# Dense products of an attention and mixture-of-experts block, issued as four column groups of 32 outputs

## The chip, the core and the metric

The kernel runs on one core of one Trainium2 chip. Its time is the device time of one launch in microseconds (us), as a median of several runs. The core has a matrix engine (PE, with its weight loads listed apart as PEld), a vector engine (DVE), a scalar engine (ACT), GpSimd (POOL) and a queue engine that issues the DMAs (SP). They run side by side and wait for each other through semaphores.

## The reference, cut to what matters

The input x has 4 sequences of 2048 tokens with 512 features, in f32. It is layer-normalized; attention with 16 heads of 32 features and a top-2-of-8 expert layer both read the normalized rows, and both results are added to x:

```python
xn  = _layernorm(x)
qkv = einsum('bnc,dc->bnd', xn, qkv_w) + qkv_b             # q, k, v: dense, 512 x 512 each
attn = softmax(einsum('bhqd,bhkd->bhqk', q, k) * 32**-0.5)
out = einsum('bhqk,bhkd->bhqd', attn, v)
a   = einsum('bnc,dc->bnd', out, proj_w) + proj_b           # dense, 512 x 512
h   = gelu(einsum('bsd,bkde->bkse', xn, W1[idx]) + b1[idx]) # dense, two experts per sequence
o   = einsum('bkse,bkef->bksf', h, W2[idx]) + b2[idx]       # dense
y   = x + a + sum(o, over the two experts) / 2
```

## The kernel before, in words

The work is cut into 1024 units. A unit is one sequence b (4), one group g of four heads (4), one chunk qc of 512 queries (4) and one tile kt of 128 keys (16). The loop over U (L638) writes one unit after the other, and each engine executes what it is given in just this order: the schedule is manual (L216), no scheduler reorders it. LEAD = 22 further units come first, with negative U. The class Plan decides beforehand which dense product goes into which unit.

In a unit PE gets, in this order:

1. `shift` (L533): four bf16 products, 32 contraction rows by 128 outputs, which put minus the row maximum into the banks of the scores.
2. `score` (L542) and `score_max` (L519): eight f32 products with 32 contraction rows and 128 outputs each, one head per 32 rows. Half of them are scores of this unit, half are for the maxima of the unit 22 later.
3. In even units `weigh` (L551): the probabilities of two units times v, eight f32 products of 128 contraction rows and 32 outputs. The four heads write to the four groups of 32 output partitions of one bank. In one even unit out of 16, `add_keys` (L579) follows in the same form: it sums the softmax denominators.
4. In odd units, transposes if there are any (`turn` L361 in f32, `turn_maxima` L616 in bf16, both with 128 rows and 128 outputs), then one dense product by `dense` (L422): q or k (`project_qk`, L405), v (`project_v`, L415), an expert's first (L436) or second layer (L446), or the output projection (L457). Some odd units have no dense product: gaps that Plan spreads over the program.

A dense product fills one bank of 128 partitions x 512 f32. Before the change it is four program matmuls of 128 contraction rows, 128 outputs and 512 columns, one for each quarter of the 512 features:

```python
for d in range(DC):
    nc.tensor.matmul(pp, w[:, d, :], xn[:, d, :], start=(d == 0), stop=(d == DC - 1))
```

One f32 program matmul appears as two weight loads and two matmuls in the trace, so a dense product has 8 loads and 8 matmuls, and a `weigh` has 16 and 16. A bf16 matmul and a transpose appear as one load and one matmul.

`weigh` already has the form that the change gives to the dense products:

```python
for n in range(2):
    for j in range(GH):
        r = rows_of(j)                                   # 32 rows: j*32 to j*32+32
        nc.tensor.matmul(acc[r, :], held["v", ...][:, (kt + n) % TPC, r], pT[u + n][:, j, :],
                         start=(n == 0), stop=(n == 1))
```

The other engines: ACT takes the exponential of the scores (L658), four per unit, and in 32 units the gelu of a whole expert tile with a table load on either side of it (L662). DVE takes the row maxima (L664), four per unit, and sums what `weigh` gives (L567). POOL sums the probabilities for the denominators, one addition per unit (L577, L575 for the first), and does the small steps of the maxima (L610, L612), the division (L629) and a bias (L682). Eight PSUM banks go round among scores, maxima, `weigh` and dense products. Probabilities have four buffers (L219), so ACT can write those of unit U only when PE and POOL are done with those of U-4.

There are 504 dense products of the kind that `dense` and the start (L502 to L505) issue: 8 in the start (q and k of the first head group), 22 in the lead and 474 in the odd units. Eight more at the end (lines 748, 756 and 763) are written apart.

Of the kernel before, what the change touches and what calls it, by code (L numbers as in the profile page):

```python
# [17 lines left out]
P = 128  # L18
HEADS = 16
HD = 32  # L20
GH = P // HD
# [165 lines left out]
def block_kernel(  # L187
# [16 lines left out]
    nc = tc.nc  # L204
    B, N, D = x.shape
    E = Wr.shape[1]
    DC = D // P
# [17 lines left out]
    def bank(name):  # L225
        return ps.tile([P, CH], F32, tag="bank", name=name)

    def rows_of(j):
        return slice(j * HD, (j + 1) * HD)
# [83 lines left out]
    first = pair.tile([B, D], F32, tag="att", name="first")  # L313
# [74 lines left out]
    nc.vector.max_index(chosen, best, scores)  # L388


    kT, qT = {}, {}
    hT, bias, b1s = {}, {}, {}

    def with_bias(dst, src, col, on_dve):
        if on_dve:
            nc.vector.tensor_scalar(dst, src, col, None, ALU.add)  # L396
        else:
            nc.scalar.activation(dst, src, AF.Identity, bias=col)  # L398

    def project_qk(kind, b, g, c, xn, w, on_dve=False):  # L400
        pp = bank(f"{kind}ps_{b}_{g}_{c}")
        t = kv_pool.tile([P, CH], F32, tag=kind, name=f"{kind}T_{b}_{g}_{c}",
                         bufs=2 * NCH if kind == "k" else NCH + 3)
        for d in range(DC):
            nc.tensor.matmul(pp, w[:, d, :], xn[:, d, :], start=(d == 0), stop=(d == DC - 1))  # L405
        col = "qk".index(kind) * DC + g
        with_bias(t, pp, bqkv[:, col : col + 1], on_dve)
        (kT if kind == "k" else qT)[b, g, c] = t

    def project_v(b, n, xn, w, U):  # L410

        c, i = divmod(n, TPC)
        pp = bank(f"vps_{b}_{n}")
        for d in range(DC):
            nc.tensor.matmul(  # L415
                pp, xn[:, d, ts(i, P)], w[:, d, :], start=(d == 0), stop=(d == DC - 1)
            )
        t = pair.tile([P, D], F32, tag="vrow", name=f"v_{b}_{n}")
        nc.vector.tensor_tensor(t, pp, bv_bc, ALU.add)
        later(U + 2, lambda: nc.sync.dma_start(v_dram[b, c][:, i, :], t))  # L420

    def dense(item, U, on_dve):  # L422
        kind, b = item[:2]
        tiles = [held[n] for n in plan.needs(item)]
        if kind in "kq":
            project_qk(kind, *item[1:], *tiles, on_dve=on_dve)
        elif kind == "v":
            project_v(*item[1:], *tiles, U)
        elif kind == "w1":
            c, k, f = item[2:]  # L430
            xn, w = tiles
            if f == 0:
                hT[k] = stream.tile([P, DC, CH], F32, tag="h", name=f"h_{b}_{c}_{k}", bufs=2)
            pp = bank(f"hps_{b}_{c}_{k}_{f}")
            for d in range(DC):
                nc.tensor.matmul(pp, w[:, d, :], xn[:, d, :], start=(d == 0), stop=(d == DC - 1))  # L436
            with_bias(hT[k][:, f, :], pp, b1s[b, k][:, f : f + 1], on_dve)
            if f == DC - 1:
                at = U + 2 if U > 0 or U == -1 else U + 1
                curves[at] = hT[k]  # L440
        elif kind == "w2":
            c, k, i = item[2:]
            w, row = tiles
            pp = bank(f"ops_{b}_{c}_{k}_{i}")
            for f in range(DC):
                nc.tensor.matmul(  # L446
                    pp, hT[k][:, f, ts(i, P)], w[:, f, :], start=(f == 0), stop=(f == DC - 1)
                )
            nc.vector.scalar_tensor_tensor(row, pp, 0.5, row, ALU.mult, ALU.add)
            if k == TOP_K - 1:  # L450
                later(U + 2, lambda: nc.sync.dma_start(part_dram[b, c, i], row))
        else:
            qc, i = item[2:]
            at, w, row = tiles
            pp = bank(f"prps_{b}_{qc}_{i}")
            for g in range(DC):
                nc.tensor.matmul(  # L457
                    pp, at[:, g, ts(i, P)], w[:, g, :], start=(g == 0), stop=(g == DC - 1)
                )
            finish(b, qc, i, pp, row, U)  # L460

    def finish(b, qc, i, pp, row, U):
        tok = qc * CH + i * P
        nc.vector.tensor_tensor(row, pp, row, ALU.add)
        later(U + 2, lambda: nc.sync.dma_start(out[b, tok : tok + P, :], row))
# [31 lines left out]
    for c in range(NCH):  # L497
        xn = load("xq", ("stage", 0, c))
        for i in range(TPC):
            turn(xn, x_first[c][:, i, :], i, f"0_{c}_{i}")  # L500
        nc.sync.dma_start(xn_dram[0, c], xn)
        if c + 1 < NCH:  # L502
            first_norm(c + 1)
        for kind in "kq":
            project_qk(kind, 0, 0, c, xn, held["w" + kind, 0])  # L505


    def place(u):
        rest, kt = divmod(u, NT)
        rest, qc = divmod(rest, NCH)  # L510
        return (*divmod(rest, DC), qc, kt)
# [4 lines left out]
    def later(u, do):  # L516
        waiting.setdefault(u, []).append(do)
# [120 lines left out]
    for U in range(-LEAD, plan.units):  # L638
# [3 lines left out]
        b, g, qc, _ = place(U) if second else (0, 0, 0, 0)  # L642
# [22 lines left out]
        last = U + LEAD  # L665
        if first_pass is not None and last % NT == NT - 1:
            where, n = place(last)[:3], last // NT
# [26 lines left out]
        for step, sb, n in plan.extra.get(U, []):  # L694
# [8 lines left out]
            else:  # L703
                c, i = divmod(n, TPC)
# [6 lines left out]
        for item in plan.items.get(U, []):  # L711
            dense(item, U, curve is not None)
# [13 lines left out]
        for n, c in ((16, NCH - 1), (1, NCH - 2)):  # L726
            if U == plan.units - n:
# [7 lines left out]
                n = DC - 1 if c == NCH - 1 else DC  # L735
# [8 lines left out]
    w = held["wb", ("proj",)]  # L744
    for i in range(TPC):
        pp = bank(f"last2_{i}")
# [6 lines left out]
    for i in range(TPC):  # L753
        pp = bank(f"last1_{i}")
# [58 lines left out]
```

## Time and profile before

| what | value |
|---|---|
| median of 3 runs | 5157.79 us (5157.7 to 5157.85) |
| the profiled execution's own time | 5157.05 us |
| its span | 5155.2 us |
| mean granted PE clock | 0.999 of full speed |
| PE busy | 5076.8 us, 98% of the span |
| POOL busy | 4515.3 us, 88% |
| DVE busy | 3449.7 us, 67% |
| ACT busy | 2520.4 us, 49% |
| matmuls, weight loads | 33924 each |
| HBM traffic | 65 GB/s over the span |

The busy time of PE counts overlapping matmuls once. In the timeline a line gives start, length, engine, line of the kernel, operation, the tiles written and read, contraction rows*outputs, and the count; "idle before" in brackets tells how long the engine sat idle and what ended it. For PEld, idle time is ordinary: a load takes less time than the matmul that it prepares.

### The profile page before, as it was taken

What the parts mean: (1) busy time and instruction counts of PE and PEld (TensorE: products, weight loads), DVE (VectorE), ACT (ScalarE), POOL (GpSimd) and SP (SyncE); (2) the same over time, 40 slices, a digit from 0 to 9 for tenths busy, and PEclk for the clock granted to TensorE, in tenths of its full rate; (3) what the DMA queues carried; (4) which work ended last, traced back from release to release, by engine and by line L of the source; (5) the groups of instructions that cost most, each with busy time, mean ns of one, the idle gap of its engine ahead of it and who ended that gap; (6) DMA issues with size and microseconds to landing.
All of it is one profiled execution on the core that took longest, in us unless ns stands there. A gap on an engine that the chain in (4) does not pass through costs nothing.

```text
span 5155.2 us, 83981 instructions
## 1 busy us (share of the span) xinstructions
PE 5076.8 (98%) x33924; PEld 2028.1 (39%) x33924; DVE 3449.7 (67%) x5495; ACT 2520.4 (49%) x4571; POOL 4515.3 (88%) x1430
## 2 busy tenths in 40 slices
PE   8999999999999999999999999999999999999998
PEld 3333333433333333443333433343333333333343
DVE  5666676766766667666766767766667666666672
ACT  1445545544544545554445454555444454555543
POOL 0699898988999989998999989989999998999992
PEclk9999999999999999999999999999999999999999
DMA  4211112301222212221121221221112211021112
GB/s 164 68 56 50 52 64 79 111 30 38 66 82 68 66 64 78 72 80 44 48 93 46 78 84 52 86 84 58 39 57 87 77 62 58 17 74 34 38 44 78
DMA packets 220580, 338.64 MB, mean 66 GB/s; under 512 B 14364, under 2 KB 129052, under 8 KB 205984
## 3 DMA queue, kind: packets, MB, share of 16 engines
q1 hardware_dynamic: 220192, 333.28, 19.2%
q8 instruction: 266, 4.36, 0.3%
q14 instruction: 122, 1.00, 0.1%
HBM read 249.61 MB, written 83.62 MB: 65 GB/s over the span
## 4 chain that ended last, share of the span: by engine, by line
PE 96%; POOL 2%; ACT 1%; DVE 1%; issue 0%; DMA 0%; SPq 0%; ACTq 0%; POOLq 0%
PE acc L558 18%; PE m L528 17%; PE s L546 17%; PE hps L436 9%; PE ops L446 9%; PE s L538 7%; PE kps L405 5%; PE vps L415 5%; PE qps L405 4%; PE prps L457 4%; POOL psum L577 2%; PE keys L583 1%; ACT L658 1%; PE xt L365 1%; ACT p L658 1%
## 5 line engine op out<-in xcount | busy, mean ns | idle before, releaser
L577 POOL TENSOR_TENSOR psum<-psum,p 128x2048 f32<-128x2048 f32 x882 | 3991.1, 4525 | 240.7 <-ACT p L658 206.3
L664 DVE TENSOR_REDUCE mx<-m 128x1 f32<-128x512 f32 x4096 | 2544.5, 684 | 1074.1 <-PE m L528 1073.3
L658 ACT ACTIVATE p<-s 128x512 f32<-128x512 f32 x4096 | 2121.8, 604 | 1811.6 <-PE m L528 1680.7
L546 PE MATMUL s<-qT,kT 32*128 32x512 f32 x8192 | 1922.5, 588 | 0.0
L528 PE MATMUL m<-kT,qT 32*128 32x512 f32 x8192 | 1908.3, 590 | 2.5 <-DVE h L396 1.4
L528 PEld LDWEIGHTS m<-kT,qT 32*128 32x128 f32 x8192 | 931.4, 184 | 323.0 <-issue 241.7
L558 PE MATMUL acc<-p,v 128*32 128x512 f32 x8192 | 990.1, 599 | 39.2 <-ACT p L658 39.2
L546 PEld LDWEIGHTS s<-qT,kT 32*128 32x128 f32 x8192 | 764.5, 185 | 30.8 <-issue 12.5
L558 PEld LDWEIGHTS acc<-p,v 128*32 128x32 f32 x8192 | 215.4, 109 | 739.1 <-ACT p L658 429.0
L436 PE MATMUL hps<-xf,w 128*128 128x512 f32 x1024 | 472.9, 604 | 0.2 <-ACT p L658 0.2
L446 PE MATMUL ops<-wb_w,h 128*128 128x512 f32 x1024 | 472.8, 604 | 0.2 <-ACT p L658 0.2
L538 PE MATMUL s<-negm,ones_b 32*128 32x512 bf16 x4096 | 420.9, 384 | 5.5 <-ACT p L658 3.5
L538 PEld LDWEIGHTS <-ones_b 32*128 32x128 bf16 x4096 | 108.7, 91 | 804.4 <-issue 797.2
L567 DVE TENSOR_TENSOR sacc<-acc,sacc 128x512 f32<-128x512 f32 x448 | 310.0, 692 | 153.6 <-PE acc L558 153.6
L575 POOL TENSOR_TENSOR psum<-p,p 128x2048 f32<-128x2048 f32 x63 | 284.6, 4517 | 132.8 <-ACT p L658 132.8
L446 PEld LDWEIGHTS ops<-wb_w,h 128*128 128x128 f32 x1024 | 184.0, 189 | 269.2 <-issue 183.7
L436 PEld LDWEIGHTS hps<-xf,w 128*128 128x128 f32 x1024 | 184.0, 189 | 268.8 <-issue 186.0
L398 ACT ACTIVATE h<-hps,b 128x512 f32<-128x512 f32 x115 | 79.2, 688 | 355.8 <-PE hps L436 355.8
L415 PE MATMUL vps<-wb_v,xq 128*128 128x512 f32 x512 | 236.8, 605 | 2.2 <-issue 2.0
L676 DVE RECIPROCAL sums<-sums 128x128 f32<-128x128 f32 x252 | 237.9, 944 | 0.7 <-ACT sums L595 0.7
L405 PE MATMUL kps<-xq,wk 128*128 128x512 f32 x480 | 221.6, 604 | 1.0 <-ACT p L658 0.2
L405 PE MATMUL qps<-xq,wq 128*128 128x512 f32 x480 | 221.5, 604 | 0.1
(89 smaller groups left out, 1839.2 us busy)
## 6 DMA issues: line engine op xcount, KB each, us to landing
xq<-xn_dram SPq DMA_DIRECT2D x64, 1024.0 KB, 5.5
w<-in_W_dram SPq DMA_DIRECT2D x128, 256.0 KB, 3.1
xn_dram<-xq_stage SPq DMA_DIRECT2D x16, 1024.0 KB, 6.4
v_dram<-v SPq DMA_DIRECT2D x64, 256.0 KB, 2.4
xf<-xn_dram SPq DMA_DIRECT2D x16, 1024.0 KB, 6.0
v<-v_dram SPq DMA_DIRECT2D x64, 256.0 KB, 4.3
row<-in_x_dram SPq DMA_DIRECT2D x64, 256.0 KB, 5.8
part_dram<-row SPq DMA_DIRECT2D x64, 256.0 KB, 2.1
```

The costliest lines, as they stand in the source:

```text
L405: nc.tensor.matmul(pp, w[:, d, :], xn[:, d, :], start=(d == 0), stop=(d == DC - 1))
L415: nc.tensor.matmul(pp, xn[:, d, ts(i, P)], w[:, d, :], start=(d == 0), stop=(d == DC - 1))
L436: nc.tensor.matmul(pp, w[:, d, :], xn[:, d, :], start=(d == 0), stop=(d == DC - 1))
L446: nc.tensor.matmul(pp, hT[k][:, f, ts(i, P)], w[:, f, :], start=(f == 0), stop=(f == DC - 1))
L528: nc.tensor.matmul(t, qT[b, g, qc][r, ts(i, P)], kT[b, g, kc][r, :], start=True, stop=True)
L538: nc.tensor.matmul(tiles[j], ones_b[r, :], negm[b, g, qc][r, :], start=True, stop=False)
L546: nc.tensor.matmul(tiles[j], kT[b, g, kt // TPC][r, ts(kt % TPC, P)], qT[b, g, qc][r, :], start=False, stop=True,)
L558: nc.tensor.matmul(acc[r, :], held["v", (b, g, kt // TPC)][:, (kt + n) % TPC, r], pT[u + n][:, j, :], start=(n == 0), stop=(n == 1),)
L567: nc.vector.tensor_tensor(t, acc, t, ALU.add)
L577: nc.gpsimd.tensor_tensor(psums[b, g, qc], psums[b, g, qc], pT[u], ALU.add)
L658: nc.scalar.activation(pT[U][:, j, :], tiles[j], AF.Exp, scale=SCALE)
L664: nc.vector.tensor_reduce(dst, t, AX.X, ALU.max, negate=True)
```

## The change

A new helper `product` issues every dense product of `project_qk`, `project_v` and `dense` as column groups: for each quarter of the contraction, four matmuls, each with 32 columns of the stationary operand and the 32 output partitions that belong to them. The moving operand of the four is the same tile. The number of program matmuls of a product goes from 4 to 16. The order of everything else, on all engines, stays as it was; so do the eight products at the end, the transposes, and the readers of the banks.

```diff
+    def product(pp, terms, last=True, first=True):
+
+        for n, (lhsT, rhs) in enumerate(terms):
+            for j in range(GH):
+                nc.tensor.matmul(
+                    pp[rows_of(j), :], lhsT[:, rows_of(j)], rhs,
+                    start=(first and n == 0), stop=(last and n == len(terms) - 1),
+                )
...
     def project_qk(kind, b, g, c, xn, w, on_dve=False):
...
-        for d in range(DC):
-            nc.tensor.matmul(pp, w[:, d, :], xn[:, d, :], start=(d == 0), stop=(d == DC - 1))
+        product(pp, [(w[:, d, :], xn[:, d, :]) for d in range(DC)])
...
     def project_v(b, n, xn, w, U):
...
-        for d in range(DC):
-            nc.tensor.matmul(
-                pp, xn[:, d, ts(i, P)], w[:, d, :], start=(d == 0), stop=(d == DC - 1)
-            )
+        product(pp, [(xn[:, d, ts(i, P)], w[:, d, :]) for d in range(DC)])
...
     def dense(item, U, on_dve):
...
-            for d in range(DC):
-                nc.tensor.matmul(pp, w[:, d, :], xn[:, d, :], start=(d == 0), stop=(d == DC - 1))
+            product(pp, [(w[:, d, :], xn[:, d, :]) for d in range(DC)])
...
-            for f in range(DC):
-                nc.tensor.matmul(
-                    pp, hT[k][:, f, ts(i, P)], w[:, f, :], start=(f == 0), stop=(f == DC - 1)
-                )
+            product(pp, [(hT[k][:, f, ts(i, P)], w[:, f, :]) for f in range(DC)])
...
-            for g in range(DC):
-                nc.tensor.matmul(
-                    pp, at[:, g, ts(i, P)], w[:, g, :], start=(g == 0), stop=(g == DC - 1)
-                )
+            product(pp, [(at[:, g, ts(i, P)], w[:, g, :]) for g in range(DC)])
```

## The prediction

> **What bounds the kernel.** I read the page first: busy times, then the chain of work that ended last.
>
> ```profile
> PE 5076.8 (98%) x33924; PEld 2028.1 (39%) x33924; DVE 3449.7 (67%) x5495; ACT 2520.4 (49%) x4571; POOL 4515.3 (88%) x1430
> ...
> PE 96%; POOL 2%; ACT 1%; DVE 1%; issue 0%; DMA 0%; SPq 0%; ACTq 0%; POOLq 0%
> PE acc L558 18%; PE m L528 17%; PE s L546 17%; PE hps L436 9%; PE ops L446 9%; PE s L538 7%; PE kps L405 5%; PE vps L415 5%; PE qps L405 4%; PE prps L457 4%; POOL psum L577 2%; PE keys L583 1%; ACT L658 1%; PE xt L365 1%; ACT p L658 1%
> ```
>
> PE carries the chain, and the dense lines (L405 to L457) are 36% of it. So what one dense product costs between its neighbours on PE is what counts. The timeline of weight loads near the end shows a dense product and, right after it, eight packs of four column groups (four of L558, four of L583): as many contraction passes as a dense product, in the form that the change gives it.
>
> ```profile
> 5078.69 0.30 PEld L457 LDWEIGHTS prps<-wb_proj,xl_at 128*128 128x128 f32 x2 [0.76 <-issue]
> ...
> 5082.32 0.10 PEld L538 LDWEIGHTS <-ones_b 32*128 32x128 bf16 x4 [0.76 <-issue]
> ...
> 5083.50 0.16 PEld L558 LDWEIGHTS acc<-p,v 128*32 128x32 f32 x8 [0.76 <-issue]
> 5083.96 0.13 PEld L558 LDWEIGHTS acc<-p,v 128*32 128x32 f32 x4 [0.30 <-issue]
> 5084.39 0.13 PEld L558 LDWEIGHTS acc<-p,v 128*32 128x32 f32 x4 [0.30 <-issue]
> 5084.82 0.13 PEld L583 LDWEIGHTS keys<-p,ones 128*32 128x32 f32 x4 [0.30 <-issue]
> ...
> 5087.07 0.10 PEld L538 LDWEIGHTS <-ones_b 32*128 32x128 bf16 x4 [0.84 <-issue]
> ```
>
> First load to the first load of what follows: 5082.32 - 5078.69 = 3.63 us for the dense product, 5087.07 - 5083.50 = 3.57 us for the packs. Both come after a drain of PE and end with one.
>
> **The change, per product.** From single start times in the trace: (a) First load to the second matmul (or pack): 535 ns dense, 455 ns for `acc`. The first load takes 0.19 us for 128 outputs, 0.11 for 32, and the four small loads run side by side. Saved: 80 ns. (b) After it, matmuls come every 429 ns in both forms. Pace: no change. (c) In a pack the four groups start 6 to 7 ns apart, so the last ends 20 ns later: +20. Sum -60 ns (3631 against 3571). The 3631 hold for 394 products that follow the 32-row scores, and alike for the other positions; the same drain (516 ns from the last matmul's start to the next load) precedes both forms.
>
> A rule speaks against (c). The Trainium skill ("TensorE: Matmul & The Clock Gate", section "Measured speedup vs the span model") has a pack last a matmul plus about 4 ns for each further tile. If that came with each of 8 packs, it would be 8 x 12 = 96 ns, more than the 80 saved: +16 ns per product. The row shows packs at 429 ns, the stagger paid once. I take the row; the rule makes the first rival.
>
> **After transposes.** 45 products follow an f32 transpose directly, 36 a bf16 one. Both are 128 rows x 128 outputs, the tiling of the old products, not of the new ones. For f32 the dense load now starts 54 ns after the last transpose matmul does: no drain. The Trainium skill ("TensorEngine Tiling (Array Packing)", section "Key Properties") says that a change of tiling mode drains PE. No row shows an f32 transpose followed by another tiling, so: a drain costs 516 - 429 = 87 ns beyond the last matmul's own pace after 512 columns; 128 columns take a quarter, 107 ns; 107 + 87 - 54 = +140 ns, net +80 per product. Bounds: 0 (no drain) and 280 (twice); I take 140, nearest to the row. For bf16:
>
> ```profile
> 1477.75 0.23 PEld L620 LDWEIGHTS <-spread 128*128 128x128 bf16 x4 [0.76 <-POOL att L629]
> 1478.19 0.30 PEld L405 LDWEIGHTS kps<-xq,wk 128*128 128x128 f32 x2 [0.21 <-ACT p L658]
> ```
>
> Here 0.44 us pass from the first transpose's load to the dense load, although the tiling is the same; before a 32-row bf16 load it is 0.33 at its usual value. So this place waits already. Bounds: the wait shrinks by 108 ns, or grows by 87; I take no change.
>
> **What lies on the path.** The 474 products in odd units and the 22 in the lead stand in PE's chain. From one `add_keys` to the next are 16 units; with eight products, no gelu and no f32 transposes such a stretch lasts 77.87 us in 15 of 17 cases, and PE has work in all of it, so PE alone sets it. In units with gelu, ACT still waits 0.36 us for PE before its table load, so 0.06 us pass through there too. In the start, 4 pairs of q and k stand between transposes: each saves the load and pays a drain; I count 0. Where POOL is the chain, the gain is lost:
>
> ```profile
> 4948.20 2.08 ACT p L658 x4
> ...
> 4950.41 4.54 POOL psum L577
> ...
> 5051.80 4.56 POOL psum L577
> ...
> 5058.75 3.63 PE prps L457 x8
> ```
>
> From 4950 to 5056 us POOL works without a wait for PE. Six dense products lie there; they gain nothing.
>
> Sum: 496 - 6 = 490, of which 45 follow f32 and 36 bf16 transposes, 409 neither. 409 x 0.0605 = 24.7; 36 x 0.0605 = 2.2; 45 x 0.080 = -3.6: 23.3 us less. From the profiled execution's 5157.05 (span 5155.2 and 1.85 around it) that makes 5133.8; the median of the runs stood 0.7 higher, so 5134.5.
>
> The costs set at nothing: evacuation by ACT and DVE reads the same bank, 20 ns later within a product that ends 60 earlier. 504 x 48 = 24192 more PE instructions are fetched; instruction queues hold 0.4% of the DMA time now. No wait is added: all four groups use one bank, and the reader waits for the last matmul.
>
> **Rivals.** (1) Stagger in each pack, by the rule above: 409 + 36 products at +0.016 and 45 at +0.156 make +14.1 us: 5172. This ends slower. It decides from 10 ns per pack (80 / 8); for it is only the rule, against it the 429 ns of packs in a row.
>
> (2) PE's instruction supply. A pair of units with a product now holds 128 loads and matmuls in 9.57 us, 75 ns each; it would be 176 in 9.51, 54 ns each. If PE's sequencer gave one per 60 ns, each of 474 pairs would take 10.56 us: +498 us, 5630. It decides from 54 ns. For it: nothing so dense runs for long. Against: from 5091.9 us on, 346 instructions ran in 18.3 us (53 ns each) at undisturbed pack pace. If PE's queue holds 64 (the figure of the first page, which no run here shows), they exclude only more than 18.3 / (346 - 64) = 65 ns. The same page's sustained rate of 81 ns for a load and a 128-column matmul would be 40 ns each, an estimate that leaves room.
>
> (3) POOL takes over, half the gain is lost: 11.6 us, 5146. POOL has 88% of the span, but ACT overwrites probabilities 5.2 us or more after POOL has read them, everywhere before 4980 us; eight products per 16 units take only 0.5 us from this, and POOL falls idle again in most of them. Unlikely outside the tail.
>
> (4) The change doesn't do what it says: the small loads don't run side by side for a shared moving tile, and products stay as long as they were; with the drains after transposes, 5158 to 5164.
>
> **How the numbers follow.** Forecast 0.72, within 5124 to 5144.5: the low end has no drain after f32 transposes (6.3) and the shorter wait after bf16 (3.9), the high end twice the drain (6.3), the longer wait (3.1) and 0.6 in the start. Rival (3) 0.06, (4) 0.08, (1) 0.05, (2) 0.05; 0.04 for a larger gain that I don't see. The range 5122 to 5147 takes in the forecast and (3), and a little of the last. A measurement of this kernel tells 0.2%, 10.3 us, from no change. Faster by more: 0.72 + 0.06 + 0.04 = 0.82; within: 0.08; slower: 0.10.
>
> **What would show it.** Right: the first loads of a product as 8 small ones within 0.16 us, packs at 0.43, 3.57 us from first load to the next L538, and stretches with eight plain products at 77.87 - 8 x 0.06 = 77.39 us. For the drain: about 0.19 us instead of 0.05 between the last f32 transpose and the product. Wrong: packs over 0.44 us (1), pauses between packs in odd units only, or loads that trickle (2), ACT waiting for L577 in mid-program (3). The forecast falls if a product's 3.57 us don't come about.

## The result and the profile after

The changed kernel takes 5134.1 us (median of 6 runs, 5133.48 to 5136.19) against 5157.82 us (6 runs, 5154.98 to 5158.59): 23.7 us less, a ratio of 0.9955 with a 95% interval of 0.9944 to 0.9967. The forecast was 5134.5. The profiled execution has a span of 5131.6 us, 23.6 below the one before.

The page's busy times and the head of its chain:

```profile
PE 5054.0 (98%) x46020; PEld 1776.4 (35%) x46020; DVE 3449.0 (67%) x5495; ACT 2516.2 (49%) x4571; POOL 4534.6 (88%) x1430
...
PE 95%; POOL 2%; ACT 1%; DVE 0%; issue 0%; DMA 0%; SPq 0%; ACTq 0%; POOLq 0%
```

12096 more matmuls and as many more weight loads, and yet PE is busy for 22.8 us less: four matmuls of four column groups, which run side by side (a pack), count as the time of one. PE still carries the chain. The timeline of weight loads shows the same output projection near the end that the prediction showed of before:

```profile
5055.06 0.16 PEld L395 LDWEIGHTS prps<-wb_proj,xl_at 128*32 128x32 f32 x8 [0.76 <-issue]
5055.52 0.13 PEld L395 LDWEIGHTS prps<-wb_proj,xl_at 128*32 128x32 f32 x4 [0.30 <-issue]
5055.95 0.13 PEld L395 LDWEIGHTS prps<-wb_proj,xl_at 128*32 128x32 f32 x4 [0.30 <-issue]
...
5058.63 0.10 PEld L536 LDWEIGHTS <-ones_b 32*128 32x128 bf16 x4 [0.84 <-issue]
```

Eight small loads come within 0.16 us, packs follow every 0.43, and 5058.63 - 5055.06 = 3.57 us pass until the next part's load. From single start times it is 3571 ns in nearly all products that follow scores, 3631 before. After f32 transposes the picture is another. The same view around one of them, before and then after:

```profile
813.07 0.42 PEld L365 LDWEIGHTS xt<-ident,xl_normal 128*128 128x128 f32 x4 [0.76 <-ACT p L658]
813.50 0.30 PEld L436 LDWEIGHTS hps<-xf,w 128*128 128x128 f32 x2
```

```profile
804.75 0.42 PEld L365 LDWEIGHTS xt<-ident,xl_normal 128*128 128x128 f32 x4 [0.76 <-ACT p L656]
805.34 0.16 PEld L395 LDWEIGHTS hps<-xf,w 128*32 128x32 f32 x8 [0.17 <-ACT p L656]
```

From the first transpose's load to the product's first load it is 0.43 us before and 0.59 after: the product now waits for the transposes. Measured from the last transpose's start, 54 ns have become 201.

Stretch by stretch (16 units, from one `add_keys` to the next) the two traces differ by 0.48 us where there are eight plain products, by 0.42 where there are seven, and by -0.55, -0.40 and -0.02 in three neighbouring stretches of each of the first three sequences: there the transposes lie, and the kernel is slower than before.

Three differences in the profiled pair belong to the clock of these two executions and not to the change. PE's granted clock became full at 22.2 us before and at 16.9 after, which shortens the start by 2.1 us, and each trace has a spell of half clock of 3.4 us in mid-program (last section) that costs 1.5 us before and 1.7 after. Together they favour the profiled execution of after by some 1.9 us, so 21.7 of its 23.6 us are left for the change.

### The profile page after: what moved, and what is told of

It is laid out like the page before. It is cut to its first block, busy times and chain, and to the rows that moved or that the text cites. A ratio compares the mean times of both kernels' runs of the same rounds, so it can differ in the third digit from the quotient of the medians.

```text
span 5131.6 us, 108175 instructions
## 1 busy us (share of the span) xinstructions
PE 5054.0 (98%) x46020; PEld 1776.4 (35%) x46020; DVE 3449.0 (67%) x5495; ACT 2516.2 (49%) x4571; POOL 4534.6 (88%) x1430
## 3 DMA queue, kind: packets, MB, share of 16 engines
q8 instruction: 361, 5.91, 0.5%
## 4 chain that ended last, share of the span: by engine, by line
PE 95%; POOL 2%; ACT 1%; DVE 0%; issue 0%; DMA 0%; SPq 0%; ACTq 0%; POOLq 0%
PE acc L556 18%; PE m L526 17%; PE s L544 17%; PE ops L395 9%; PE hps L395 9%; PE s L536 7%; PE kps L395 4%; PE vps L395 4%; PE qps L395 4%; PE prps L395 4%; POOL psum L575 2%; PE keys L581 1%; ACT L656 1%; PE xt L365 1%; ACT p L656 1%; PE mt L618 0%
## 5 line engine op out<-in xcount | busy, mean ns | idle before, releaser
L575 POOL TENSOR_TENSOR psum<-psum,p 128x2048 f32<-128x2048 f32 x882 | 4008.6, 4545 | 217.3 <-ACT p L656 182.1
L395 PE MATMUL hps<-xf,w 128*32 128x512 f32 x4096 | 466.0, 595 | 0.2 <-ACT p L656 0.2
L395 PE MATMUL ops<-wb_w,h 128*32 128x512 f32 x4096 | 466.0, 595 | 0.2 <-ACT p L656 0.2
L395 PE MATMUL vps<-wb_v,xq 128*32 128x512 f32 x2048 | 233.0, 595 | 2.3 <-issue 2.0
L395 PEld LDWEIGHTS ops<-wb_w,h 128*32 128x32 f32 x4096 | 120.0, 109 | 317.6 <-issue 229.8
L395 PEld LDWEIGHTS hps<-xf,w 128*32 128x32 f32 x4096 | 120.0, 109 | 317.1 <-issue 232.1
L395 PE MATMUL kps<-xq,wk 128*32 128x512 f32 x1920 | 218.4, 595 | 1.0 <-ACT p L656 0.2
L395 PE MATMUL qps<-xq,wq 128*32 128x512 f32 x1920 | 218.4, 595 | 0.1
```

What stands on the lines that cost most here:

```text
L395: nc.tensor.matmul(pp[rows_of(j), :], lhsT[:, rows_of(j)], rhs, start=(first and n == 0), stop=(last and n == len(terms) - 1),)
L575: nc.gpsimd.tensor_tensor(psums[b, g, qc], psums[b, g, qc], pT[u], ALU.add)
```

## The experiments

All times are medians; ratios are to the kernel before, on the same chip.

**1. The old form after f32 transposes.** Products in units with f32 transposes keep their four wide matmuls (unless a bf16 transpose lies between); all else is as in the changed kernel.

```diff
+    plain = [False]
+
     def product(pp, terms, last=True, first=True):
 
+        if plain[0]:
+            for n, (lhsT, rhs) in enumerate(terms):
+                nc.tensor.matmul(
+                    pp, lhsT, rhs,
+                    start=(first and n == 0), stop=(last and n == len(terms) - 1),
+                )
+            return
...
+        turned = any(step == "turn" for step, _, _ in plan.extra.get(U, []))
+        plain[0] = turned and not (last % NT == 3 and NT < last <= plan.units + 3)
         for item in plan.items.get(U, []):
```

> Products that directly follow f32 transposes (45 of them) keep the old form of 128 outputs, all others are four column groups. Theory: the column form gains 60 ns per product but pays a drain after an f32 transpose, because the tiling changes there (201 ns instead of 54 from the last transpose's start to the first load). So these 45 products get 147 - 60 = 87 ns shorter each: 3.9 us less than the changed kernel, about 5130.2 us. Stretches of 16 units that hold such transposes gain 0.3 to 0.6 us against the changed kernel, all others nothing. Rival: the 147 ns are not the change of tiling but a cost of the transposes' neighbours in any form; then these 45 products lose the 60 ns that they had gained, and the kernel takes 5136.8 us.

Measured: 5129.82 us (5 runs, 5129.62 to 5133.15), ratio 0.9948, interval 0.9935 to 0.9962. The intervals of this kernel and of the changed one overlap, so the 4.3 us between the medians rest on the trace. There the transposes run into the product again:

```profile
805.13 0.42 PEld L365 LDWEIGHTS xt<-ident,xl_normal 128*128 128x128 f32 x4 [0.76 <-ACT p L665]
805.57 0.30 PEld L397 LDWEIGHTS hps<-xf,w 128*128 128x128 f32 x2
```

0.44 us instead of 0.59. The three stretches of each sequence gain 0.62, 0.45 and 0.27 us against the changed kernel, 4.0 us over three sequences, and all other stretches agree within 0.02 us. From the last transpose's start to the first load it is 51 ns again. So the 147 ns belong to the change of tiling between transpose and product, and the rival, which had the kernel at 5136.8 us, falls. By the traces this version is faster than both kernels.

**2. Two groups of 64 outputs.**

```diff
-            for j in range(GH):
+            for j in range(2):
+                half = slice(j * 64, j * 64 + 64)
                 nc.tensor.matmul(
-                    pp[rows_of(j), :], lhsT[:, rows_of(j)], rhs,
+                    pp[half, :], lhsT[:, half], rhs,
```

> Every dense product as two column groups of 64 outputs. Theory: the gain is the shorter first weight load less the stagger of the groups at the end. Loads of 32 and 128 outputs take 109 and 189 ns, so 64 take about 136: 53 ns saved, one step of stagger (7 ns) paid, 3585 ns per product instead of 3631 (and 3571 with four). 445 products gain 46 ns, 45 after f32 transposes lose 101: about 16 us less than before, 5142 us. Rival: the gain comes from four groups that share the array in another way than one wide matmul does (a faster pace of the packs); then two groups bring half of it or nothing, and the interval of 429 ns between packs differs between two groups, four groups and one.

Measured: 5143.51 us (8 runs), ratio 0.9973, interval 0.9963 to 0.9984. The weight loads of a product:

```profile
2506.58 0.20 PEld L396 LDWEIGHTS vps<-wb_v,xq 128*64 128x64 f32 x4 [0.76 <-ACT p L657]
2507.07 0.14 PEld L396 LDWEIGHTS vps<-wb_v,xq 128*64 128x64 f32 x2 [0.29 <-issue]
2507.49 0.14 PEld L396 LDWEIGHTS vps<-wb_v,xq 128*64 128x64 f32 x2 [0.28 <-issue]
...
2510.17 0.10 PEld L537 LDWEIGHTS <-ones_b 32*128 32x128 bf16 x4 [0.81 <-issue]
```

A load of 64 outputs takes 0.14 us, packs come every 0.43 as with one group and with four, and the product takes 2510.17 - 2506.58 = 3.59 us; single start times say 3584 ns, where 3585 were expected. The gain follows the width of the first load, less the stagger, and the rival of a faster pace falls. After f32 transposes the first load again comes at 201 ns: two groups are also another tiling than the transposes'.

**3. Group by group.** The same matmuls, with the loops over groups and contraction exchanged.

```diff
-        for n, (lhsT, rhs) in enumerate(terms):
-            for j in range(GH):
+        for j in range(GH):
+            for n, (lhsT, rhs) in enumerate(terms):
```

> The same 16 program matmuls per product in another order: all four quarters of the contraction for the first 32 outputs, then for the second, and so on. Theory: matmuls start in program order, and those of one column group wait for each other; groups run side by side only where neighbours in the program belong to different groups. Each product then takes 32 matmuls of 429 ns, about 13.9 us, 10.3 us more: 504 times this is 5190 us, so about 10.3 ms. Rival: PE finds matmuls of free groups in its queue, and the order doesn't matter: 3.57 us per product, 5134 us.

Measured: 7749.19 us (one run). Neither expectation holds. The timeline of PE shows a product of 8.79 us to the next part:

```profile
3002.24 8.86 PE L395 MATMUL hps<-xf,w 128*32 128x512 f32 x32
3011.03 0.39 PE L536 MATMUL s<-negm,ones_b 32*128 32x512 bf16 x4
```

8.79 - 3.57 = 5.22 us more, and 504 times this is 2631 us: 5134 + 2631 = 7765, near the measured time. The starts of the 32 matmuls of one product, in ns from its first load, tell how it comes about:

```
2, 455, 884, 1314, (1743, 1749), (2172, 2202), (2601, 2631), (3030, 3060),
(3489, 3495), (3919, 3949), (4348, 4378), (4777, 4807), (5236, 5242), (5665, 5695), (6094, 6124), (6524, 6554),
6983, 7412, 7841, 8270
```

Four single starts, twelve pairs, four single starts: 20 steps of 429 ns instead of 32 (strict order) or 8 (free choice). A group has eight matmuls; when its fifth starts, the first of the next group starts beside it. The trace does not name the group of a matmul. The counts fit a line of its own for each column group, where one matmul runs and three wait, while the fifth that finds the line full holds up everything behind it in the program.

**4. Blocks that fit such a line.** Two quarters of the contraction, four trace matmuls, for each group in turn; then the other two.

```diff
-        for n, (lhsT, rhs) in enumerate(terms):
-            for j in range(GH):
-                nc.tensor.matmul(
+        for h in range(0, len(terms), 2):
+            for j in range(GH):
+                for n in (h, h + 1):
+                    lhsT, rhs = terms[n]
+                    nc.tensor.matmul(
```

> The 16 program matmuls of a product in blocks: two quarters of the contraction (4 matmuls of the trace) for each group in turn, then the other two quarters for each group. Theory from the group-by-group run, where the next group began when the running one had four matmuls left: one matmul of a group runs, three wait in a line of that group's own, and only a fifth holds up the program behind it. Four in a row then hold up nothing: all groups start at once, and only the change to the second block may show a load that is not ahead (30 ns in that run): 3.57 to 3.7 us per product, 5134 to 5185 us. Rival: PE looks a fixed four matmuls ahead of the oldest that hasn't ended; then two groups at most run together, a product takes over 6 us, and the kernel over 6.3 ms.

Measured: 5153.0 us (12 runs), ratio 0.9992, interval 0.9983 to 1.0. The timeline of PE:

```profile
2504.16 3.68 PE L397 MATMUL vps<-wb_v,xq 128*32 128x512 f32 x32
2507.77 0.39 PE L538 MATMUL s<-negm,ones_b 32*128 32x512 bf16 x4
```

A product takes 3.61 us, 38 ns more than in the changed kernel, where a fixed look-ahead would have it over 6. The groups start 13 ns apart instead of 6.7, and the last matmul starts 58 ns after the first of its pack instead of 20. So a fixed look-ahead is excluded, and the lines of four foretold this run; a longer line would fit it too, and the four rests on experiment 3. At the same time 496 x 0.038 = 19 us, nearly the whole gain of the change, are lost to the order of the same instructions.

**5. and 6. How many instructions PE can take.** The columns in halves, then in quarters, each part with its own loads.

```diff
+        for e in range(2):
+            half = slice(e * 256, e * 256 + 256)
...
-                    pp[rows_of(j), :], lhsT[:, rows_of(j)], rhs,
+                        pp[rows_of(j), half], lhsT[:, rows_of(j)], rhs[:, half],
```

> Every product in two halves of 256 columns, each with its own 32 loads and 32 matmuls: 64 and 64 per product instead of 32 and 32, for the same columns streamed. Theory: PE's instruction supply has room; packs come every 214 ns, and the product takes 3.56 us (241 to the second pack, 14 x 214, 20 of stagger, 301 to the next load): 5130 to 5145 us. A pair of units then takes 240 instructions in 9.5 us, 40 ns each. Rival: the supply ends between 54 and 40 ns per instruction; at 45 ns a pair takes 10.8 us, and the kernel is about 600 us slower; the packs of a product's second half come at the supply's pace of 8 instructions, not at 214 ns.

Measured with halves: 5144.91 us (12 runs), ratio 0.9976, interval 0.9968 to 0.9985. The product takes 3591 ns, 33 more than expected (2 ns per pack), and 496 x 0.020 = 9.9 us account for most of the distance to the changed kernel (10.8).

> Every product in four parts of 128 columns: 128 loads and 128 matmuls per product for the same columns, four times as many as in the changed kernel. A search for the end of the instruction supply, which 40 ns per instruction (the run with halves) didn't reach. If neither supply nor loads bind, packs come every 107 ns and the product takes about 3.6 us, 14 ns per instruction; but a load of 32 outputs takes 109 ns, about as long as the pack, so 3.6 to 4.2 us is what I expect of loads alone (5150 to 5450 us). If the supply ends between 20 and 40 ns, the product takes 5 to 10 us, and the kernel 5.8 to 8.4 ms.

Measured with quarters: 5181.31 us (one run). The timeline of PE:

```profile
2500.16 3.70 PE L397 MATMUL kps<-xq,wk 128*32 128x128 f32 x128
2503.79 0.39 PE L538 MATMUL s<-negm,ones_b 32*128 32x512 bf16 x4
```

128 matmuls and 128 loads go through in 3.63 us, 14 ns per instruction, with packs every 109 ns; the lasting rate of a pair of units is 368 instructions in 9.6 us, 26 ns each. No steady limit of the supply was found. The 109 ns are as long as one load of 32 outputs takes; that the load sets them was not tested by itself. The products are 60 ns longer than in the changed kernel, which makes 30 of the 47 us between the two. Ten products at full clock are longer still, by 0.1 to 1.9 us each and 8 us together, most of them by one pause between their loads; after the start, no product of the changed kernel has that. The instruction queue moved 12.11 MB here and 5.91 in the changed kernel, so a late fetch would fit, but what the pauses wait for is not shown.

## Why the prediction was right, point by point

- **(a) and (c), the saving of 80 ns and the stagger of 20.** Predicted 3571 ns per product, measured 3571. With two groups the same two terms give 3585, measured 3584. The gain is the first weight load of a product, which nothing hides after a drain. All later loads lie under running matmuls in both forms.
- **(b), the pace.** 429 ns with one, two and four groups. The stagger is paid once, as the row said. The rule of the Trainium skill ("TensorE: Matmul & The Clock Gate", section "Measured speedup vs the span model"), if its 4 ns for each further tile came in every pack, would have given 3.65 us per product and rival (1). No product shows it.
- **After f32 transposes.** Predicted +140 ns for the drain (194 from the last transpose's start), measured 147 (201). Experiment 1 takes it away and gets 4.0 us back. The term was 45 x 0.080 = 3.6 us; it measured 45 x 0.087 = 3.9.
- **After bf16 transposes.** Predicted no change of the wait, by a choice between two bounds. For 32 of the 36 products that is so: the median is 254 ns after, 256 before. In both traces their load comes 50 to 52 ns after the end of an ACT exponential, so the wait is for ACT, as the row in the prediction names it (`0.21 <-ACT p L658`), and the drain lies inside it. The other four don't wait for ACT (one is in the lead, three come where f32 transposes stand before the bf16 ones). Their load came 2 ns after the last transpose's start before, and comes 148 ns after it now: +146 ns each, 0.6 us in all, which the prediction did not have. Experiment 1 left these four as they are.
- **The start.** Counted as 0. A pair of q and k from one `kps` to the next takes 10.24 us after and 10.15 before, 0.1 us more each, 0.4 in all. The first product of a pair is 80 ns shorter, but the transposes behind the second one now load 0.52 us after its last matmul starts, and not at once. Most of that is made up before the next pair; how was not followed up.
- **The tail.** Of the nine products in the two stretches from the `add_keys` at 4930.2 us (4906.6 after) to the last that follows a sum, six were to gain nothing, which leaves 0.2 us. The stretches differ by 0.31 and -0.35 us: nothing together. The missing 0.2 is POOL's: from the addition where it last sits idle (4950.41 before, 4926.68 after) to the start of its last one it takes 106.02 us before and 106.25 after, since its additions became slower (last section).
- **Rival (2), the instruction supply.** Excluded for this change: it decides from 54 ns, and 14 ns were seen within a product. This was the costliest rival, and the trace of before could only bound it at 65 ns.
- **Rival (3), POOL.** ACT shows no wait for L575 before the tail, and the stretches that took 77.87 us take 77.39, the value that was named.
- **Rival (4).** Falls with the 3571 ns.

The sum by the measured terms is 409 x 0.060 + 36 x 0.060 - 45 x 0.087 - 4 x 0.146 - 0.4 = 21.8 us, less 0.2 in the tail. The profiled pair leaves 21.7 for the change (23.6 less 1.9 of clock), and the prediction had 23.3. So the mechanism and its main terms were right, some 1.6 us of small costs were missed, and a gain of clock of about the same size hid that in the profiled pair. How much clock lies in the 23.7 between the medians is not known, and the interval of the ratio (17 to 29 us) is wider than any of this: the agreement to 0.4 us is partly luck, and the terms are what was tested.

## What to carry to other kernels

In this kernel PE goes back and forth between tilings, and a dense product behind the scores pays a drain (516 ns from the last matmul's start to the next load) and one weight load that nothing hides (189 ns for 128 outputs, 109 for 32). A product with the full 128 outputs gains from four column groups because that first load gets shorter, not because more of the array works: the pace stays at 429 ns. Look at what stands before the product: if it had the old tiling, as the transposes here, the narrower form buys a drain that costs more (147 ns) than it saves (60), so choose the form product by product. Within the column form keep neighbours in the program on different groups, contraction outside and groups inside; the reverse order made a product 2.5 times as long.

## What the hardware showed that was not expected

**Lines per column group.** A matmul of a free group starts ahead of up to three that wait for a busy one (experiments 3 and 4). It is read from the counts of starts: 20 steps of 429 ns in experiment 3, and 3.61 us per product in experiment 4.

**POOL's additions became slower.** The same L575 addition of 128 x 2048 takes 4545 ns on average after and 4525 before; with two groups it takes 4534, group by group 4516:

```profile
L575 POOL TENSOR_TENSOR psum<-psum,p 128x2048 f32<-128x2048 f32 x882 | 4008.6, 4545 | 217.3 <-ACT p L656 182.1
```

The traces place it beside the products. Additions with more than 3 us of a dense product beside them take 4515 ns before (102 of them), 4533 with two groups (127) and 4557 with four (134); those with none beside them take 4532, 4533 and 4537. The number of instructions is not the reason: with quarters, which have four times as many per product, the mean is 4545 as well. That PE's reading of the moving tile once per group disturbs POOL's reads would fit, but was not tested. Only in the tail does it cost time, the 0.2 us above.

**Half clock after short pauses of PE.** In the changed kernel's trace PE sits idle for 1.5 us at 3270.4 us. The table of windows (start and end, length, PE busy, then the other engines, PEclk, DMA share, GB/s) shows what follows:

```profile
3269.00:3273.00 4.00, 2.50 (x20) 0.68 (x16) 3.72 (x6) 3.79 (x6) 2.17 (x3) 1.00 1.04 343
3273.00:3277.00 4.00, 4.00 (x25) 1.03 (x28) 1.72 (x4) 1.35 (x3) 2.57 (x1) 0.57 0.05 13
3277.00:3281.00 4.00, 4.00 (x40) 1.33 (x36) 2.68 (x5) 2.76 (x5) 2.96 (x2) 1.00 0.01 4
```

For 3.4 us the granted clock is half, and a `weigh` takes 3.45 us instead of 1.92. The trace of before has one such spell at 797 us, after pauses of 1.1 and 0.8 us. The same place in the trace of after, with pauses of 1.2 and 0.8 us, has none, and neither has the place at 3288 us of before, with a pause of 1.4 us. So it comes and goes with the execution, which is why stretches and not whole spans were compared. What decides it is not shown; over 30 single pauses of 1.16 us in either trace were followed by no such spell.

The trace of after has a second spell in the tail, at 5024 us, behind a pause of 2.9 us. POOL carries the chain there, and it costs nothing that can be seen: in experiment 1 the spell at this place lasts 6.8 us instead of 3.4, and the stretch takes the same time to 0.01 us.
